# Statistics further ahead in stage 1, x loaded before the constants, and the output gate computed 16 rows ahead across the border to stage 3

## The chip, the core and the metric

The kernel runs on one core of a Trainium2 chip. The core has a matrix engine (TensorE, PE in the profile), a vector engine (VectorE, DVE), an activation engine (ScalarE, ACT), a general engine (GpSimd, POOL) and a queue engine that issues transfers (SyncE, SP). Each engine works through its own instructions in order, and the engines wait for one another through semaphores. The metric is the device time of one execution in microseconds (us); lower is better. A change counts as faster or slower here when the time moves by more than 2%.

## The reference, cut to what matters

x has 384 x 384 positions of 128 channels. Two layers are applied to it, in float32.

```python
# layer 0
z = layernorm(x)
left  = (z @ Wl + bl) * sigmoid(z @ Wlg + blg)
right = (z @ Wr + br) * sigmoid(z @ Wrg + brg)
core  = einsum('bikh,bjkh->bijh', left, right)      # for each channel h a 384x384x384 product
zo    = layernorm(core) @ Wout + bout
x     = x + sigmoid(x @ Wg + bg) * zo               # the gate uses the x that came in

# layer 1, on the new x (called pair)
left      = pair @ W_left + b_left + pair @ W_eq + b_eq
right_sum = sum over the row of (pair @ W_right + b_right)
gate      = sigmoid(pair @ W_gate + b_gate)
out       = (left * right_sum * gate) @ W_out + b_out
x         = layernorm(out + pair)
```

The gate `sigmoid(x @ Wg + bg)` of layer 0 needs only the kernel's input, not `core`.

## The kernel before

It has three stages, one after the other.

**Start.** 28 small loads (weights, biases) go out on SyncE's queue, the weights are folded with the norms' scales, and only then the first loads of x are issued.

**Stage 1** goes over x in 144 chunks of 8 rows of 128 positions. A chunk is two steps of four rows. Per step: statistics on VectorE, 1/sqrt(var+eps) by a power chain on GpSimd (once a chunk), scaling on GpSimd, four transposes on TensorE, four projections onto 512 columns, a sigmoid on ScalarE, a product on VectorE. Slices of the result go to DRAM.

```python
AHEAD = NQ + 3                       # NQ = 2 steps a chunk
def stats(n, q, half):
    for r in range(r0, r0 + 2):
        seq(nc.vector.bn_stats(st[:, r, :], loaded[n][:, r, :]))
    for r in range(r0, r0 + 2):
        seq(nc.vector.bn_aggr(mv[:, r, :], st[:, r, :]))
    if q == NQ - 1 and half == 1:    # the power chain, once a chunk
        seq(nc.gpsimd.tensor_scalar(rs, mv[:, :, 1], EPS, 1.0, ALU.add, ALU.mult))
        seq(nc.gpsimd.tensor_tensor(rs, rs, mhalf[:, :XR], ALU.pow))
        seq(nc.gpsimd.tensor_tensor(sh, mv[:, :, 0], rs, ALU.mult))
        seq(nc.gpsimd.tensor_scalar(sh, sh, -1.0, 1.0, ALU.mult, ALU.add))
...
for k, (n, q) in enumerate(steps):
    if k + 2 < len(steps):
        zs[k + 2] = scale(*steps[k + 2])          # GpSimd, four rows of z
    for half in range(2):
        back(n, q, zt, half)                      # projections, sigmoid, product
        if half == 0 and k + 1 < len(steps):
            ahead = front(zs.pop(k + 1))          # transposes, copy
        if k + AHEAD < len(steps):
            stats(*steps[k + AHEAD], half)
    ...
```

`seq` keeps an instruction behind those that were written before it for the same engine.

**Stage 2** goes over the 128 channels: 9 matmul pairs each, a copy to SBUF, the square, two running sums, and a store of `core`. After it, `rstd` is computed for three blocks of 128 rows, on VectorE and ScalarE (a square root), and stored.

**Stage 3** goes over 384 rows in a software pipeline. `tick(t)` works on row t-d for several delays d:

```python
# d=1: gate matmul, sigmoid           d=0: three transposes of x, copy, cs = core * rstd
# d=2: pr matmul, two vector ops      d=3: two matmuls, sigmoid, vector op
# d=6: wo on ScalarE                  d=7: six py matmuls, statistics
# d=9: normalize on ScalarE           d=10: scale and shift, store every 4 rows
load_rows(0); load_rows(RG)           # x, core and rstd of 4 rows each
for t in range(N + D):                # D = 10
    ...
    tick(t)
```

Of the kernel before, what the change touches and what calls it, by code (L numbers as in the profile page):

```python
# [19 lines left out]
def triangle_then_gated_row_kernel(ctx: ExitStack, tc: tile.TileContext, a: dict, out: bass.AP):  # L20
# [20 lines left out]
    RG = 4  # L41

# [10 lines left out]

    def const(shape, name):
        return cpool.tile(shape, F32, tag=name, name=name)

    def load(dst, src):
        nc.sync.dma_start(out=dst, in_=src)
# [11 lines left out]
    ident = const([P, P], "ident")  # L70
    make_identity(nc, ident)
    avg = const([P, P], "avg")
    nc.vector.memset(avg, 1.0 / P)
    mhalf = const([P, 16], "mhalf")
    nc.vector.memset(mhalf, -0.5)

    g0, b0 = column("L0_conv_norm_g"), column("L0_conv_norm_b")
    go, bo = column("L0_conv_onorm_g"), column("L0_conv_onorm_b")
    wout0, bout0 = matrix("L0_conv_Wout"), column("L0_conv_bout")
    wg0, bg0 = matrix("L0_conv_Wg"), column("L0_conv_bg")  # L80
    wleft, bleft = matrix("L1_conv_W_left"), column("L1_conv_b_left")
    weq, beq = matrix("L1_conv_W_eq"), column("L1_conv_b_eq")
    wright, bright = matrix("L1_conv_W_right"), column("L1_conv_b_right")
    wgate, bgate = matrix("L1_conv_W_gate"), column("L1_conv_b_gate")
    wout1, bout1 = matrix("L1_conv_W_out"), column("L1_conv_b_out")
    lns, lnb = const([P, C], "lns"), const([P, C], "lnb")
    load(lns, a["L1_conv_ln_scale"].partition_broadcast(P))
    load(lnb, a["L1_conv_ln_bias"].partition_broadcast(P))

    wz = const([P, 4 * H], "wz")  # L90
    wc = const([P, C], "wc")
    bz = const([P, 1], "bz")
    with tc.tile_pool(name="prep", bufs=1) as pp, tc.tile_pool(name="prep_ps", bufs=1, space=PSUM) as ps:

        wst, wcat = pp.tile([P, 4 * H], F32, name="wst"), pp.tile([P, 4 * H], F32, name="wcat")
        bst, bcat = pp.tile([1, 4 * H], F32, name="bst"), pp.tile([1, 4 * H], F32, name="bcat")
        for n, (w, b) in enumerate((("Wl", "bl"), ("Wr", "br"), ("Wlg", "blg"), ("Wrg", "brg"))):
            load(wst[:, n * H:(n + 1) * H], a["L0_conv_" + w])
            load(bst[:, n * H:(n + 1) * H], a["L0_conv_" + b].rearrange("(o h) -> o h", o=1))
        for t, st in ((wcat, wst), (bcat, bst)):  # L100
            for g in range(2):
                nc.vector.tensor_copy(
                    t[:, g * 2 * H:(g + 1) * 2 * H].rearrange("p (h s) -> p s h", s=2),
                    st[:, g * 2 * H:(g + 1) * 2 * H].rearrange("p (s h) -> p s h", s=2),
                )

        d = pp.tile([P, 1], F32, name="d")
        nc.vector.tensor_sub(d, b0, g0)  # L110
        m1 = pp.tile([P, P], F32, name="m1")
        nc.vector.tensor_scalar(m1, avg, d, None, ALU.mult)
        p1 = ps.tile([P, 4 * H], F32, name="p1")
        nc.tensor.matmul(p1, lhsT=m1, rhs=wcat, start=True, stop=False)
        nc.tensor.matmul(p1, lhsT=avg[0:1, :], rhs=bcat, start=False, stop=True)
        nc.vector.scalar_tensor_tensor(wz, wcat, g0, p1, ALU.mult, ALU.add)


        m2 = pp.tile([P, P], F32, name="m2")
        nc.vector.tensor_scalar(m2, avg, go, -1.0, ALU.mult, ALU.mult)  # L120
        p2 = ps.tile([P, C], F32, name="p2")
        nc.tensor.matmul(p2, lhsT=m2, rhs=wout0, start=True, stop=True)
        nc.vector.scalar_tensor_tensor(wc, wout0, go, p2, ALU.mult, ALU.add)
        p3 = ps.tile([P, 1], F32, name="p3")
        nc.tensor.matmul(p3, lhsT=wout0, rhs=bo, start=True, stop=True)
        nc.vector.tensor_add(bz, p3, bout0)


        nc.vector.tensor_add(wleft, wleft, weq)
        nc.vector.tensor_add(bleft, bleft, beq)  # L130
        p4 = ps.tile([P, 3], F32, name="p4")
        for n, w in enumerate((wleft, wgate, wright)):
            nc.tensor.matmul(p4[:, n:n + 1], lhsT=w, rhs=bout1, start=True, stop=True)
        for n, b in enumerate((bleft, bgate, bright)):
            nc.vector.tensor_sub(b, b, p4[:, n:n + 1])
        nc.vector.tensor_scalar(bright, bright, float(N), None, ALU.mult)


    chunks = [(kb, ig, c) for kb in range(NB) for ig in range(NG) for c in range(G // XR)]
    kept = {(NB - 1, ig): None for ig in range(NG - KEEP, NG)}  # L140
    with ExitStack() as ctx2:
# [15 lines left out]
        with tc.tile_pool(name="p1x", bufs=6) as xp, tc.tile_pool(name="p1w", bufs=3) as wp, \  # L157
             tc.tile_pool(name="p1s", bufs=5) as sp, \
# [3 lines left out]
            AHEAD = NQ + 3  # L162
# [13 lines left out]

            def stats(n, q, half):

# [10 lines left out]
                if q == NQ - 1 and half == 1:  # L189
                    seq(nc.gpsimd.tensor_scalar(rs, mv[:, :, 1], EPS, 1.0, ALU.add, ALU.mult))  # L190
                    seq(nc.gpsimd.tensor_tensor(rs, rs, mhalf[:, :XR], ALU.pow))  # L191
                    seq(nc.gpsimd.tensor_tensor(sh, mv[:, :, 0], rs, ALU.mult))
                    seq(nc.gpsimd.tensor_scalar(sh, sh, -1.0, 1.0, ALU.mult, ALU.add))
# [56 lines left out]
            for n in range(6):  # L250
                load_chunk(n)
# [3 lines left out]
            zs = {k: scale(*steps[k]) for k in range(2)}  # L255
            zt = front(zs.pop(0))
            for k, (n, q) in enumerate(steps):
                ahead = None
                if k + 2 < len(steps):
                    zs[k + 2] = scale(*steps[k + 2])  # L260
                for half in range(2):
                    back(n, q, zt, half)
                    if half == 0 and k + 1 < len(steps):
                        ahead = front(zs.pop(k + 1))
                    if k + AHEAD < len(steps):
                        stats(*steps[k + AHEAD], half)
# [4 lines left out]
                store_slice()  # L271
                if k == len(steps) - 2 * G // 4 + 16:
# [5 lines left out]
        spool = ctx2.enter_context(tc.tile_pool(name="stats", bufs=1))  # L278
        with tc.tile_pool(name="p2out", bufs=3) as op, tc.tile_pool(name="p2sq", bufs=2) as qp, \
             tc.tile_pool(name="p2ps", bufs=2, space=PSUM) as ps:  # L280
# [34 lines left out]
        with tc.tile_pool(name="rstd", bufs=2) as rp:  # L315
            for b in range(NB):
                m2, ve, r0, r1 = (rp.tile([P, N], F32, tag=t, name=t) for t in ("m2", "ve", "r0", "r1"))
                nc.vector.scalar_tensor_tensor(m2, csum[:, b], 1.0 / (H * H), csum[:, b], ALU.mult, ALU.mult)
                nc.vector.scalar_tensor_tensor(ve, csq[:, b], 1.0 / H, m2, ALU.mult, ALU.subtract)
                nc.vector.tensor_scalar(ve, ve, 0.0, EPS, ALU.max, ALU.add)  # L320
                nc.scalar.activation(r1, ve, AF.Sqrt)
                nc.vector.reciprocal(r0, r1)
                nc.vector.tensor_mul(r1, r0, r0)
                nc.vector.scalar_tensor_tensor(r1, r1, -0.5, ve, ALU.mult, ALU.mult)
                nc.vector.scalar_tensor_tensor(r1, r1, 1.5, r0, ALU.add, ALU.mult)
                nc.sync.dma_start(out=rstd_d[b * P:(b + 1) * P, :], in_=r1)

    with tc.tile_pool(name="p3in", bufs=3) as inp, tc.tile_pool(name="p3out", bufs=3) as op, \
         tc.tile_pool(name="p3w", bufs=4) as wp, tc.tile_pool(name="p3l", bufs=7) as lp, \
         tc.tile_pool(name="p3s", bufs=4) as sp, \
         tc.tile_pool(name="p3ps", bufs=4, space=PSUM) as ps, \
         tc.tile_pool(name="p3ps2", bufs=4, space=PSUM) as ps2:
# [8 lines left out]

        nc.vector.tensor_scalar(lns, lns, -1.0, None, ALU.mult)
        lnsb = lns.unsqueeze(1).to_broadcast([P, NB, C])
        lnbb = lnb.unsqueeze(1).to_broadcast([P, NB, C])
        loaded, rows, yts, pair, quad = {}, {}, {}, {}, {}

        def load_rows(i0):  # L350
            if i0 < N:
                xt = inp.tile([P, RG, NB, C], F32, tag="xt", name="xt")
                seq(nc.sync.dma_start(out=xt, in_=x[i0:i0 + RG].rearrange("i (b p) c -> p i b c", p=P)))
                ct = inp.tile([P, RG, N], F32, tag="ct", name="ct")
# [6 lines left out]
                loaded[i0] = xt, ct, rt  # L361

        D = 10

        def tick(t):

            r = [rows.get(t - d) for d in range(D + 1)]
            if r[1]:

                pg = bank("pg")  # L370
                seq(nc.tensor.matmul(pg[:, :N], lhsT=wg0, rhs=r[1]["xT"], start=True, stop=True))  # L371
                gT = r[1]["gT"] = work("gT")
                seq(nc.scalar.activation(gT, pg[:, :N], AF.Sigmoid, bias=bg0))
            if r[0]:
# [128 lines left out]
```

## Time and profile before

The time is 3588.69 us, the median of three runs (3588.11 to 3588.82). The profiled execution has a span of 3585.8 us.

| stretch of the profiled execution | us | TensorE counted busy |
| --- | --- | --- |
| start, until the first projection at 30.2 us | 30.2 | |
| stage 1, 30.0 to 1238.5 | 1208.5 | 1180.1 |
| stage 2, 1239.9 to 2020.0 | 780.1 | 779.8 |
| border, 2019.7 to 2039.4 | 19.7 | 0.9 |
| stage 3, 2060 to 3550 | 1490.0 | 1490.0 |
| after the last matmul, 3571.9 to 3586.0 | 14.1 | 0.0 |

In the lines that follow below, a timeline's columns are the start and the duration in us, the engine, the line of the kernel, the operation, what it writes and reads, and how often; in brackets the idle time before it and what ended it. PE is TensorE, SPq SyncE's queue. In a list of waits the columns are the total in us, the number of times and the longest. TensorE's busy time is to be read with care, since the ends of matmuls are modelled: a start is better evidence than a duration.

### The profile page before, as it was taken

To read this page: it belongs to the slowest core of one execution; us is meant where nothing else is said; L and a number is where in the kernel's file an instruction comes from. 1 tells how busy PE (TensorE), PEld (TensorE's weight loads), DVE (VectorE), ACT (ScalarE), POOL (GpSimd) and SP (SyncE) were. 2 spreads that over 40 slices of the span, in tenths; PEclk is the share of its full clock that TensorE was granted. 3 is DMA by queue.
4 is the path that set the end of the run, shared out by engine and by line. 5 is a ranking of instruction groups with operands and counts; after the bars stand their busy time and mean duration, and the time that the engine had idled before them with its cause. 6 is when DMAs were issued, how large, how long until landed. Compare 5 with 4: busy or idle time off the path is not lost.

```text
span 3585.8 us, 48072 instructions
## 1 busy us (share of the span) xinstructions
PE 3496.5 (98%) x13646; PEld 2102.3 (59%) x13646; DVE 2357.0 (66%) x7498; ACT 1962.6 (55%) x3815; POOL 1997.5 (56%) x3526
## 2 busy tenths in 40 slices
PE   7999999999999999999999799999999999999997
PEld 3444444444444455555555477777777777777775
DVE  4666666666666544444444588888888888888886
ACT  2444444444444333333333377777777777777776
POOL 4666666666666500000000167777777777777776
PEclk9999999999999999999999899999999999999999
DMA  3675675675675288888888766666666666666662
GB/s 86 178 222 164 182 219 162 183 219 162 186 219 158 76 271 268 270 268 273 270 266 271 240 197 205 194 201 204 194 202 199 198 203 198 199 203 196 202 203 89
DMA packets 885056, 726.00 MB, mean 202 GB/s; under 512 B 18484, under 2 KB 823352, under 8 KB 884792
## 3 DMA queue, kind: packets, MB, share of 16 engines
q1 hardware_dynamic: 884792, 722.94, 65.2%
q8 instruction: 110, 1.80, 0.2%
q14 instruction: 154, 1.26, 0.1%
HBM read 437.07 MB, written 285.80 MB: 202 GB/s over the span
## 4 chain that ended last, share of the span: by engine, by line
PE 73%; POOL 16%; DVE 6%; ACT 3%; issue 2%; DMA 0%; SPq 0%; POOLq 0%; DVEq 0%; ACTq 0%
PE pc L299 22%; PE pr L233 7%; PE pr L405 7%; PE py L434 7%; PE pg L371 7%; PE pl L420 7%; PE pg L419 7%; POOL z L201 7%; POOL rs L191 7%; PE pxt L378 4%; PE py L435 3%; DVE lr L237 3%; ACT sg L235 2%; DVE st L186 2%; PE pt L210 1%
## 5 line engine op out<-in xcount | busy, mean ns | idle before, releaser
L233 PE MATMUL pr<-wz,zt 128*128 128x512 f32 x2304 | 1038.9, 594 | 0.7 <-ACT zt L212 0.7
L299 PE MATMUL pc<-lrh 128*128 128x384 f32 x2304 | 779.8, 499 | 1.4 <-DVE lr L237 1.4
L237 DVE TENSOR_TENSOR lr<-pr,sg 128x512 f32<-128x512 f32 x576 | 398.3, 691 | 471.6 <-ACT sg L235 471.6
L235 ACT ACTIVATE sg<-pr 128x512 f32<-128x512 f32 x576 | 344.0, 597 | 643.3 <-PE pr L233 327.7
L233 PEld LDWEIGHTS pr<-wz,zt 128*128 128x128 f32 x2304 | 424.1, 194 | 415.0 <-issue 414.0
L299 PEld LDWEIGHTS pc<-lrh 128*128 128x128 f32 x2304 | 446.9, 194 | 334.5 <-DVE lr L237 2.2
L455 ACT ACTIVATE py<-py,nm,rs 128x128 f32<-128x128 f32 x1152 | 495.5, 430 | 117.2 <-POOL rs L449 90.3
L201 POOL TENSOR_SCALAR z<-xt,rs,sh 128x128 f32<-128x128 f32 x1152 | 500.4, 458 | 0.0
L308 DVE TENSOR_TENSOR csum<-csum,ct 128x1152 f32<-128x1152 f32 x128 | 173.8, 1358 | 445.0 <-ACT ct L305 445.0
L290 POOL COPY lrh<-lr 128x128 f32<-128x128 f32 x256 | 68.1, 296 | 705.4 <-issue 694.4
L434 PEld LDWEIGHTS py<-wo,u 128*128 128x128 f32 x2304 | 378.5, 191 | 105.9 <-ACT py L455 2.9
L382 POOL TENSOR_TENSOR cs<-ct,rt 128x384 f32<-128x384 f32 x384 | 384.1, 1001 | 46.6 <-DMA rt<-rstd_d 40.8
L305 ACT COPY ct<-pc 128x1152 f32<-128x1152 f32 x128 | 143.3, 1120 | 486.3 <-PE pc L299 486.3
L434 PE MATMUL py<-wo,u 128*128 128x128 f32 x2304 | 404.5, 275 | 4.3 <-ACT py L455 2.7
L391 POOL TENSOR_TENSOR yt<-yt,lnb 128x384 f32<-128x384 f32 x384 | 384.0, 1000 | 5.1 <-DVE yt L388 5.1
L440 DVE BATCH_NORM_STATS2 st<-py 128x6 f32<-128x128 f32 x1152 | 266.1, 286 | 114.7 <-PE py L435 114.7
L371 PE MATMUL pg<-xT,mat_L_conv_Wg 128*128 128x384 f32 x768 | 313.3, 490 | 11.8 <-ACT xT L380 11.8
L405 PE MATMUL pr<-cs,wc 128*128 128x384 f32 x768 | 319.8, 498 | 0.0
L406 DVE SCALAR_TENSOR_TENSOR pr<-pr,bz,gT 128x384 f32<-128x384 f32 x384 | 240.2, 625 | 116.6 <-PE pr L405 116.0
L435 PE MATMUL py<-ident,x1T 128*128 128x128 f32 x1152 | 314.7, 273 | 0.0
L419 PE MATMUL pg<-x1T,mat_L_conv_W_gate 128*128 128x384 f32 x768 | 310.5, 486 | 0.0
L420 PE MATMUL pl<-x1T,mat_L_conv_W_left 128*128 128x384 f32 x768 | 310.5, 486 | 0.0
(85 smaller groups left out, 4778.1 us busy)
## 6 DMA issues: line engine op xcount, KB each, us to landing
lr_d<-lr SPq DMA_DIRECT2D x128, 1024.0 KB, 9.1
lrh<-lr_d SPq DMA_DIRECT2D x128, 768.0 KB, 4.9
xt<-in_x_dram SPq DMA_DIRECT2D x144, 512.0 KB, 5.2
core_d<-ct SPq DMA_DIRECT2D x128, 576.0 KB, 6.2
xt<-in_x_dram SPq DMA_DIRECT2D x96, 768.0 KB, 5.0
ct<-core_d SPq DMA_DIRECT2D x96, 768.0 KB, 8.8
rt<-rstd_d SPq DMA_DIRECT2D x96, 768.0 KB, 6.3
out_dram<-yt SPq DMA_DIRECT2D x96, 768.0 KB, 4.1
```

Source lines behind the costliest of these rows:

```text
L201: seq(nc.gpsimd.tensor_scalar(z[:, r, :], xt[:, rr, :], rs[:, rr:rr + 1], sh[:, rr:rr + 1], ALU.mult, ALU.add))
L233: seq(nc.tensor.matmul(pr[:, r, :], lhsT=zt[:, 2 * half + r, :], rhs=wz, start=True, stop=True))
L235: seq(nc.scalar.activation(sg, pr[:, :, 2 * H:], AF.Sigmoid))
L237: seq(nc.vector.tensor_tensor(t[:, :, i0:i0 + 2, :], pr[:, :, :2 * H].rearrange("k i (h s) -> k h i s", s=2), sg.rearrange("k i (h s) -> k ...
L299: seq(nc.tensor.matmul(pc[:, ib, :N], lhsT=t[:, kb, ib * P:(ib + 1) * P, 0], rhs=t[:, kb, :, 1], start=(kb == 0), stop=(kb == NB - 1),))
L371: seq(nc.tensor.matmul(pg[:, :N], lhsT=wg0, rhs=r[1]["xT"], start=True, stop=True))
L405: seq(nc.tensor.matmul(pr[:, :N], lhsT=wc, rhs=r[2]["cs"], start=True, stop=True))
L419: seq(nc.tensor.matmul(pg2[:, :N], lhsT=wgate, rhs=r[3]["x1T"], start=True, stop=True))
L420: seq(nc.tensor.matmul(pl[:, :N], lhsT=wleft, rhs=r[3]["x1T"], start=True, stop=True))
L434: seq(nc.tensor.matmul(py[:, s], lhsT=r[7]["u"][:, s], rhs=r[7]["wo"], start=True, stop=False))
L435: seq(nc.tensor.matmul(py[:, s], lhsT=r[7]["x1T"][:, s], rhs=ident, start=False, stop=True, is_transpose=True))
L455: seq(nc.scalar.activation(py[:, s], py[:, s], AF.Identity, bias=nm[:, n, b:b + 1], scale=rs[:, n, b:b + 1]))
```

## The change

It has five parts:

1. In stage 1 the statistics run one step further ahead (`AHEAD = NQ + 4`), and the power chain is taken out of `stats` and put behind the scaling of its step, one step after the statistics that it reads. It is meant to keep GpSimd from waiting for VectorE with finished work behind it.
2. The first six loads of x are issued before anything else, and the constants are loaded through ScalarE's queue, those of stage 1 first. The folding of the weights for stage 3 is moved into stage 1, after its step 20.
3. In stage 3 the transposes of x and the gate run 16 rows ahead of the rest (A = 16), so that they can start before `rstd` is there. x is loaded apart from core and rstd. The pipeline becomes D = 26 ticks long.
4. `rstd` is computed inside stage 3, after row 4, in two passes over the three blocks, and stored through GpSimd's queue.
5. The pools of stages 2 and 3 wait for the tiles whose bytes they take over, not for the whole pool before them (`reuse_waits="tile"`), and lie on the other side of SBUF where that is needed. The output of the last four rows is stored row by row.

The diff, cut to its core ("..." where lines are left out):

```diff
+    A = 16
...
     def load(dst, src):
-        nc.sync.dma_start(out=dst, in_=src)
+        seq(nc.scalar.dma_start(out=dst, in_=src))
...
-            AHEAD = NQ + 3
+            AHEAD = NQ + 4
...
+            for n in range(6):
+                load_chunk(n)
...  (the constants of stage 1, ident, avg, the folding of wz)
+            def weights():
+                seq(nc.vector.scalar_tensor_tensor(wz, wcat, g0, p1[:, 0], ALU.mult, ALU.add))
...  (the loads of the other constants)
+            def late_weights():
+                ps = tps.tile([P, 4, P], F32, tag="pt", name="pw")
+                m2 = wp.tile([P, 4, C], F32, tag="z", name="m2")[:, 0]
+                seq(nc.vector.tensor_scalar(m2, avg, go, -1.0, ALU.mult, ALU.mult))
+                seq(nc.tensor.matmul(ps[:, 0], lhsT=m2, rhs=wout0, start=True, stop=True))
+                seq(nc.vector.scalar_tensor_tensor(wc, wout0, go, ps[:, 0], ALU.mult, ALU.add))
...
+                for n, (w, b) in enumerate(((wleft, bleft), (wgate, bgate), (wright, bright))):
+                    p4 = ps[:, 2, n:n + 1]
+                    seq(nc.tensor.matmul(p4, lhsT=w, rhs=bout1, start=True, stop=True))
+                    seq(nc.vector.tensor_sub(b, b, p4))
...
-                if q == NQ - 1 and half == 1:
+            def powers(n, q):
+                if q == NQ - 1:
+                    _, mv, rs, sh = normed[n]
                     seq(nc.gpsimd.tensor_scalar(rs, mv[:, :, 1], EPS, 1.0, ALU.add, ALU.mult))
...
             for k in range(AHEAD):
                 for half in range(2):
                     stats(*steps[k], half)
-            zs = {k: scale(*steps[k]) for k in range(2)}
-            zt = front(zs.pop(0))
+                if k == 1:
+                    weights()
+                if k < AHEAD - 1:
+                    powers(*steps[k])
+                if k == 1:
+                    zs = {j: scale(*steps[j]) for j in range(2)}
+                    zt = front(zs.pop(0))
             for k, (n, q) in enumerate(steps):
                 ahead = None
                 if k + 2 < len(steps):
                     zs[k + 2] = scale(*steps[k + 2])
+                if k + AHEAD - 1 < len(steps):
+                    powers(*steps[k + AHEAD - 1])
...
+                if k == 20:
+                    late_weights()
...
+        with tc.tile_pool(name="p2out", bufs=3, side="right", reuse_waits="tile") as op, \
+             tc.tile_pool(name="p2ps", bufs=2, space=PSUM, reuse_waits="tile") as ps:
...
+        xip, fp, inp, op = pool("p3x", 4), pool("p3f", A + 4), pool("p3in", 3), pool("p3out", 3)
...
+        def rstd():
...  (for all three blocks: variance on VectorE, square root on ScalarE; then for all three:)
+                seq(nc.vector.reciprocal(m, r))
...
+                seq(nc.gpsimd.dma_start(out=rstd_d[b * P:(b + 1) * P, :], in_=r))
...
-        D = 10
+        D = A + 10
...  (in tick: gate at delay 1 and transposes at delay 0 as before, cs at delay A,
...   everything else at its old delay plus A)
-        load_rows(0)
-        load_rows(RG)
+        for i0 in range(0, 4 * RG, RG):
+            load_x(i0)
         for t in range(N + D):
+            if t == 5:
+                rstd()
+                load_core(0)
+                load_core(RG)
...
+            if i >= N - RG:
+                seq(nc.sync.dma_start(
+                    out=y[i].rearrange("(b p) c -> p b c", p=P), in_=yts[N - RG][:, i % RG]
+                ))
```

## The prediction, made before the change was run

> **What bounds the kernel now.** I read the page's busy table first, then the slices, then the timeline of TensorE inside each stage, and last the list of waits. The busy table says that TensorE works all the time:
>
> ```profile
> PE 3496.5 (98%) x13646; PEld 2102.3 (59%) x13646; DVE 2357.0 (66%) x7498; ACT 1962.6 (55%) x3815; POOL 1997.5 (56%) x3526
> ```
>
> If that were true there would be 2% to win. But a matmul's end is modelled, so I looked at starts. The timeline of TensorE in the middle of stage 1:
>
> ```profile
> 503.52 1.24 PE L210 MATMUL pt<-ident,z 128*128 128x128 f32 x4
> 504.60 3.60 PE L233 MATMUL pr<-wz,zt 128*128 128x512 f32 x8
> 508.03 0.60 PE L210 MATMUL pt<-ident,z 128*128 128x128 f32 x4
> 508.47 3.60 PE L233 MATMUL pr<-wz,zt 128*128 128x512 f32 x8
> 511.90 1.23 PE L210 MATMUL pt<-ident,z 128*128 128x128 f32 x4
> 512.97 3.60 PE L233 MATMUL pr<-wz,zt 128*128 128x512 f32 x8
> ```
>
> The first column is the start, the second the duration. Eight projections take 3.43 us from start to the next group, always. Four transposes take 0.44 us from their start to the projections (508.03 to 508.47) in one step and 1.08 us (503.52 to 504.60) in the next. The long ones are counted as busy and are in truth waiting in between. The timeline of all engines there shows that z is written at one row per 0.44 us by POOL, just ahead of each transpose. Why POOL is late stands in the waits of stage 1 (30 to 1238 us):
>
> ```profile
> POOL rs L190 <- DVE mv L188: 349.6, 142, 6.7
> ```
>
> 142 times, once a chunk, POOL stands still for 2.46 us (349.6/142) at the power chain (four operations, 508.54 to 511.02, so 2.5 us), because the statistics end late on DVE; the z rows that TensorE needs next are queued behind that chain. A chunk is two steps: 8.38 us (508.03 to 516.41 in the same timeline). Without the wait it would be 2 x (0.44 + 3.43) = 7.74 us. So 0.64 us per chunk is lost.
>
> Stage 2 has nothing of the kind: 128 channels in 780 us (1239.9 to 2020), 6.09 us each, TensorE dense. Stage 3 neither: four rows take 15.85 us (3.96 each), and TensorE has no idle time from 2060 to 3550. Left are the start, where the first projection comes at 30.2, the border to stage 3, and the drain of some 14 us after the last matmul (3571.8 of 3585.8). The timeline of the start and of the border, cut:
>
> ```profile
> 13.16 30.59 SPq L172 DMA_DIRECT2D xt<-in_x_dram  x8
> 27.74 1.78 PE L210 MATMUL pt<-ident,z 128*128 128x128 f32 x4 [8.85 <-POOL z L201]
> 30.20 3.78 PE L233 MATMUL pr<-wz,zt 128*128 128x512 f32 x4 [0.68 <-ACT zt L212]
> ...
> 2021.36 0.43 SPq L353 DMA_DIRECT2D xt<-in_x_dram  x1
> 2027.34 0.88 PE L378 MATMUL pxt<-ident,xt 128*128 128x128 f32 x3 [7.63 <-DMA xt<-in_x_dram]
> 2039.43 1.65 PE L371 MATMUL pg<-xT,mat_L_conv_Wg 128*128 128x384 f32 x2 [11.21 <-ACT xT L380]
> 2042.28 1.65 PE L371 MATMUL pg<-xT,mat_L_conv_Wg 128*128 128x384 f32 x2 [0.57 <-ACT xT L380]
> 2044.36 1.56 PE L405 MATMUL pr<-cs,wc 128*128 128x384 f32 x2
> ```
>
> The first x load is issued only at 13.16, behind 28 constant loads. At the border TensorE waits 7.6 us for x and 11.2 us because ScalarE's copy stands behind the third square root, and it then runs at half rate.
>
> **What the Trainium skill says.** (1) "TensorE: Matmul & The Clock Gate", Part 1: after an idle window of about 3.4 us the array is gated to half its clock, and about as long a busy spell frees it. The trace agrees: the gate's matmul pair takes 1.65 us at 2039.4 and 0.81 us in steady state, and recovery takes some 6 us here. (2) The same page's table at the top: the queues of ScalarE, VectorE and GpSimd are strict FIFO. The trace agrees: finished x rows do not overtake the power chain on POOL. So order alone can cure stage 1. (3) The same page, Part 4: a transpose does not count as TensorE activity for that gate. No view of this trace shows it; it matters for a rival below. (4) "Trainium Kernel Development and Optimization", Key Constraints: loads issued from several engines share the same DMA engines, so a second issuer saves issue time only. Here a constant costs 0.43 us of issue on SyncE, and that is just what stands ahead of x.
>
> **The change part by part.**
>
> *Stage 1's order.* Statistics run one step further ahead (lead 6 instead of 5), and the power chain for a chunk is placed behind the scaling of its step and one step after its statistics. I count time in steps of 3.87 us. DVE ends a step's statistics about half a step after TensorE has left that step (508.45 against about 506.3). Under the new order the chain in even step k needs statistics of step k-1, ready at k+0.55; it takes 0.63 steps, so until about k+1.15; the z rows behind it take 0.45 steps, until k+1.6; TensorE wants them at k+2.45. That is 0.85 steps, over 3 us, of slack where there was a deficit of 0.64 us. POOL's work per chunk is 8 x 0.44 + 2.5 = 6.0 of 7.74 us; DVE's is 4 x 1.3 = 5.2; ScalarE's about 3.6. Nothing else becomes the bound. The gain: (1233 - 43)/8.38 = 142 chunks x 0.64 = **-90 us**.
>
> *x before constants.* Loads of x go out at about 0.7 us instead of 13.16. The projection then waits for: ten constants issued on ScalarE's queue (0.7 + 10 x 0.47 = 5.4), landed by about 8.5 (2 us as before, 1 more for the x traffic); the copies and m1, 9.2; statistics of two steps 2.35, so 11.6; chain 2.5, so 14.1; first z, cold transposes and copy (27.23 to 30.20 before, 3.0 us), so about 17. Against 30.2: **-13 us**.
>
> *Late weights.* The preparation for stage 3, which lay in the wait at the start, now comes at step 20 in the middle of a dense stage: six small matmuls and ten DVE operations in turns, in one PSUM bank. TensorE first waits for DVE to finish its backlog of half a step, about 2 us, then some five round trips of 0.6 to 1 us (at 4.53 to 5.60 the first one took 1.1). I put it at **+7 us**.
>
> *Border to stage 2.* The 1.4 us wait for the last write of lr can go, since PSUM waits by tile: **-1 us**.
>
> *Border to stage 3.* The first x load is still issued behind the last store of core (program order on SyncE), so the 7.6 us stay. Then gate and transposes of rows 0 to 15 run, with the rstd work after row 4, and the first main-path matmul (pr) comes in tick 18. In these ticks TensorE has only 0.33 + 0.65 = 0.98 us of work, but there is a chain: gate matmul to sigmoid 0.84, sigmoid to copy 0.48, copy 0.48, to the next matmul 0.05, so 1.85 us (starts at 2160.77, 2161.61 and 2162.09 in steady state). About four cold ticks at 2.85 (2039.43 to 2042.28) and twelve at 1.85 are 33.6; tables and three square roots 4; ticks 17 and 18 some 3 us more; less half a tick for the first. So pr of row 0 comes about 7.6 + 39 = 47 us after stage 2's end, against 24.6 before (2044.36 - 2019.7): +22 us. The rstd results are long there by then. It is paid back at the end: the last 16 rows need no gate and no transposes. TensorE would need 2.98 us a row; DVE needs about 3.4 (3.9 less its waits of 0.3 + 0.3), so 16 x 0.55 = -9 us. The last store is per row, 192 KB instead of 768 KB: -2 to -3 us. Together **+10 us**: the work is moved into a place where TensorE idles, but at ScalarE's pace and at the price of a later start of the main path.
>
> Sum: 3588.7 - 90 - 13 + 7 - 1 + 10 = **3502 us**, of which stage 1 ends near 1145, stage 2 near 1926.
>
> **The rivals.** *A new wait in stage 1 takes back much of the 90 us.* For it: stores and loads already saturate the DMA in half of each group (348 GB/s at 516 to 520), the group shrinks from 67 to 62 us, and statistics want x a step earlier. Against: landing of x takes 10.8 us at most, the load goes out when POOL has finished with the buffer, about six steps (23 us) ahead, and the other half of the group is nearly free (10 to 130 GB/s). It would give some 3530. *The gate runs fast.* If the 16 rows went at TensorE's own 0.98 us, the border would be about 14 us shorter, and the whole near 3485; the strict order sigmoid, copy on ScalarE speaks against it. *The gate runs cold.* With TensorE half idle, and transposes not counted, the clock may stay at half: 12 more ticks at +1.0, so 3514. *Throttling of a denser stage 1*: stage 3 is dense for 1490 us at a granted clock of 1.00, so no.
>
> **Range and chances.** Stage 1's gain is read directly from starts and I give it +-5; start and late weights together +-7, the border +-12. So 3480 to 3525. The 2% line is 3517; it takes a cold border and a slow start together, or a new wait in stage 1, to miss it: faster by over 2% 0.87, within 0.12, slower 0.01.
>
> **What will show it.** In stage 1 every group of transposes should stand 0.44 us ahead of its projections, a chunk take 7.75 us, and the wait of POOL for DVE shrink. The first projection should start near 17. A gap of several us should stand once, some 100 us in. After stage 2 a row of gate matmuls at 1.8 to 2.9 us spacing should precede the first pr by some 35 us or more, and the last 16 rows should go at about 3.4 us. It is wrong if transposes still wait every second step, if DVE waits for x, or if the border is shorter than before.

## The result, and the profile after

The changed kernel takes 3529.38 us (median of four runs, 3527.08 to 3531.18) against 3588.76 us for the kernel before. The ratio is 0.9834, with a 95% interval of 0.9817 to 0.9851: 1.7% faster, so within 2%. The prediction was 3502 us with a range of 3480 to 3525; the result lies above the range, 27 us above the estimate.

The page's busy table of the changed kernel again gives TensorE 98% of a now shorter span:

```profile
PE 3460.8 (98%) x13646; PEld 2109.6 (60%) x13646; DVE 2355.9 (67%) x7498; ACT 1946.6 (55%) x3815; POOL 1994.4 (57%) x3529
```

As before, this row tells nothing. The starts do. TensorE's timeline in the middle of stage 1 (start, duration, engine, line, operation):

```profile
502.25 0.60 PE L226 MATMUL pt<-ident,z 128*128 128x128 f32 x4
502.68 3.60 PE L249 MATMUL pr<-wz,zt 128*128 128x512 f32 x8
506.12 0.60 PE L226 MATMUL pt<-ident,z 128*128 128x128 f32 x4
506.56 3.60 PE L249 MATMUL pr<-wz,zt 128*128 128x512 f32 x8
```

Every group of transposes now stands 0.44 us ahead of its projections; the long ones of 1.08 us are gone, and a step takes 3.87 us. Yet GpSimd's wait for the statistics has shrunk by only a quarter. From the list of waits of stage 1 (total us, times, longest), the line that answers to "349.6, 142, 6.7":

```profile
POOL rs L206 <- DVE mv L199: 264.9, 141, 9.7
```

GpSimd still stands still for 1.9 us in every chunk. What changed is when the wait ends. GpSimd's timeline, the chain's first operation and the z rows behind it, before (first two lines) and after:

```profile
508.54 0.20 POOL L190 TENSOR_SCALAR rs<-mv 128x8 f32<-128x8 f32 x1 [2.43 <-DVE mv L188]
511.01 3.47 POOL L201 TENSOR_SCALAR z<-xt,rs,sh 128x128 f32<-128x128 f32 x8
...
502.75 0.20 POOL L206 TENSOR_SCALAR rs<-mv 128x8 f32<-128x8 f32 x1 [1.82 <-DVE mv L199]
505.21 3.46 POOL L217 TENSOR_SCALAR z<-xt,rs,sh 128x128 f32<-128x128 f32 x8
```

Before, the first four rows behind the chain (from 511.01) were those of the transposes at 511.90, so TensorE waited for them. Now the first four rows (from 505.21) are those of the transposes at 509.99, and the last of them is written 3.0 us earlier. GpSimd's own order has not changed: from the third chain on, each chain has the same number of z rows ahead of it in both traces (12, then 8 more each time). Taking the chain out of `stats` only kept its place there while the statistics moved ahead. So it is VectorE's lead over the chain, one step more, that made the wait harmless.

The start, in the timeline of all engines of the changed kernel (x goes out first, on SPq; the constants on ACTq, of which the first eight are shown in part):

```profile
0.72 24.35 SPq L106 DMA_DIRECT2D xt<-in_x_dram  x7
2.31 0.31 ACTq L58 DMA_DIRECT2D stage<-in_L_conv_br_dram  x1
5.22 0.34 ACTq L58 DMA_DIRECT2D stage<-in_L_conv_Wlg_dram  x1
9.08 0.33 ACTq L58 DMA_DIRECT2D stage<-in_L_conv_Wrg_dram  x1
15.06 0.69 DVE L133 COPY stage<-stage 128x256 f32<-128x256 f32 x3 [7.38 <-DMA stage<-in_L_conv_Wrg_dram]
24.64 3.78 PE L249 MATMUL pr<-wz,zt 128*128 128x512 f32 x4 [1.15 <-ACT zt L228]
```

The constants' issue is held up twice (2.31 to 5.22, 5.60 to 9.08), and the last weight, issued at 9.08, is there only just before 15.06. VectorE works in order, so the statistics of x, which stand behind these copies, start only at 16.05. The first projection starts at 24.64 instead of 30.20. ScalarE's queue as such is not slow: from 2 to 14 us the DMA engines move 238 to 298 GB/s, from 14 to 16 us 12 GB/s, and from 15.09 on the same queue issues a constant about every 0.48 us.

TensorE's timeline at step 20, where the late weights stand in the middle of stage 1, cut:

```profile
106.57 0.60 PE L226 MATMUL pt<-ident,z 128*128 128x128 f32 x4
107.01 1.88 PE L249 MATMUL pr<-wz,zt 128*128 128x512 f32 x4
111.13 0.46 PE L171 MATMUL pw<-mat_L_conv_Wout,m 128*128 128x128 f32 x2 [2.24 <-issue]
...
115.37 3.66 PE L249 MATMUL pr<-wz,zt 128*128 128x512 f32 x4
118.87 0.60 PE L226 MATMUL pt<-ident,z 128*128 128x128 f32 x4
```

From the transposes at 106.57 to these at 118.87 it is 12.3 us instead of 3.87, a hole of 8.4 us. It ends with projections at half rate: four in 3.66 us, where four took 1.88 at 107.01.

And the border to stage 3, TensorE's timeline, cut:

```profile
1939.96 0.87 PE L418 MATMUL pxt<-ident,xt 128*128 128x128 f32 x3 [7.92 <-DMA xt<-in_x_dram]
1941.73 1.65 PE L410 MATMUL pg<-xT,mat_L_conv_Wg 128*128 128x384 f32 x2 [0.90 <-ACT xT L420]
1943.17 0.85 PE L418 MATMUL pxt<-ident,xt 128*128 128x128 f32 x3
1944.59 1.65 PE L410 MATMUL pg<-xT,mat_L_conv_Wg 128*128 128x384 f32 x2 [0.57 <-ACT xT L420]
...
1989.49 1.65 PE L410 MATMUL pg<-xT,mat_L_conv_Wg 128*128 128x384 f32 x2 [0.57 <-ACT xT L420]
1992.35 1.65 PE L410 MATMUL pg<-xT,mat_L_conv_Wg 128*128 128x384 f32 x2 [0.57 <-ACT xT L420]
1994.42 1.49 PE L453 MATMUL pr<-cs,wc 128*128 128x384 f32 x2
```

A pair of gate matmuls takes 1.65 us in the first tick and still 1.65 in the last, 0.81 in steady state (from the pair's start to the next group's, 1.44 us against 0.64): the clock stays at half ("cold" below, against "warm" for full) through all 16 rows, at 2.86 us a tick. The view of busy time by stretches says the same. Its columns are the stretch, its length, the busy time of TensorE, its weight loads, VectorE, ScalarE and GpSimd with their instructions, then the granted clock, the DMA share and GB/s:

```profile
1939.96:1994.40 54.44, 41.81 (x93) 21.75 (x94) 12.82 (x13) 22.65 (x41) 5.74 (x7) 0.50 0.63 194
```

TensorE is counted busy for 41.81 of 54.44 us there, at a granted clock of 0.50.

The balance, each term the difference of two starts in the two profiled executions (spans 3585.8 and 3525.9):

| from ... to | before | after | change | predicted |
| --- | --- | --- | --- | --- |
| start to first projection | 30.20 | 24.64 | -5.6 | -13 |
| first projection to stage 2 (its start at 1239.92, 1152.24) | 1209.7 | 1127.6 | -82.1 | -90 + 7 - 1 |
| stage 2 | 779.8 | 779.8 | 0 | 0 |
| stage 2's end to row 0's main path (2019.71 to 2044.36; 1932.04 to 1994.42) | 24.6 | 62.4 | +37.7 | +22 |
| from there to the end | 1541.4 | 1531.5 | -9.9 | -11 to -12 |

The sum is -59.9, the difference of the spans. Of the last line, 2.4 us lie after the last matmul (11.7 us instead of 14.1), where the last rows are now stored one by one.

### The profile page after: what moved, and what is told of

Same layout as the page of the kernel before. It is cut to its first block, busy times and chain, and to the rows that moved or that the text cites. A ratio compares the mean times of both kernels' runs of the same rounds, so it can differ in the third digit from the quotient of the medians.

```text
span 3525.9 us, 48083 instructions
## 1 busy us (share of the span) xinstructions
PE 3460.8 (98%) x13646; PEld 2109.6 (60%) x13646; DVE 2355.9 (67%) x7498; ACT 1946.6 (55%) x3815; POOL 1994.4 (57%) x3529
## 4 chain that ended last, share of the span: by engine, by line
PE 96%; DVE 1%; ACT 1%; DMA 1%; issue 0%; POOL 0%; ACTq 0%; POOLq 0%; SPq 0%
PE pr L249 28%; PE pc L325 22%; PE pg L410 8%; PE pr L453 7%; PE py L485 7%; PE pg L469 7%; PE pl L470 7%; PE pxt L418 4%; PE pt L226 4%; PE py L486 3%; DMA xt<-in_x_dram 1%; ACT py L507 0%; PE pq L443 0%; POOL rs L496 0%; ACT xT L420 0%
## 5 line engine op out<-in xcount | busy, mean ns | idle before, releaser
L325 PE MATMUL pc<-lrh 128*128 128x384 f32 x2304 | 779.8, 499 | 1.4 <-DVE lr L253 1.4
L249 PEld LDWEIGHTS pr<-wz,zt 128*128 128x128 f32 x2304 | 416.6, 191 | 415.5 <-issue 414.1
L410 PE MATMUL pg<-xT,mat_L_conv_Wg 128*128 128x384 f32 x768 | 326.7, 508 | 12.6 <-ACT xT L420 12.6
```

The costliest lines, as they stand in the source:

```text
L249: seq(nc.tensor.matmul(pr[:, r, :], lhsT=zt[:, 2 * half + r, :], rhs=wz, start=True, stop=True))
L325: seq(nc.tensor.matmul(pc[:, ib, :N], lhsT=t[:, kb, ib * P:(ib + 1) * P, 0], rhs=t[:, kb, :, 1], start=(kb == 0), stop=(kb == NB - 1),))
L410: seq(nc.tensor.matmul(pg[:, :N], lhsT=wg0, rhs=r["xT"], start=True, stop=True))
```

## The experiments

The question was which of the five parts carries the gain, and what at the border and the start eats 30 us of it. Theory A: the clock stays at half because TensorE has gaps in the ticks with gate work alone. Theory B: the chain over ScalarE or rstd sets the border's length and the clock only follows. Executions of one and the same kernel differ by up to some 5 us (stage 2, with the same matmuls and waits, takes 783.6 us instead of 779.8 in the profiled execution of two of these runs), so differences of a few us are read from the traces.

### The order of stage 1 alone

```diff
 # the kernel before
-            AHEAD = NQ + 3
+            AHEAD = NQ + 4
     (power chain out of stats into powers(n, q), as in the change)
+                if k + AHEAD - 1 < len(steps):
+                    powers(*steps[k + AHEAD - 1])      # behind scale(k + 2)
```

> The kernel before with the new order of stage 1 alone (statistics one step further ahead, power chain behind the scaling). If that order is the whole gain, the time falls by 90 us or more, to about 3498, below the changed kernel's 3529, and the other four parts together cost 30 us. If the x loads first or the new pools carried part of the gain, it stays above 3529.

Measured: 3495.18 us, ratio 0.9741 (0.9727 to 0.9756). This one part is faster than the whole change by 34 us. Its first projection starts at 27.64 (the first power chain no longer waits for all statistics), stage 2 at 1146.49, so stage 1 takes 1118.9 us instead of 1209.7: 90.9 us less. The lines of these two starts:

```profile
27.64 3.78 PE L235 MATMUL pr<-wz,zt 128*128 128x512 f32 x4 [0.68 <-ACT zt L214]
...
1146.49 13.81 PE L306 MATMUL pc<-lrh 128*128 128x384 f32 x40 [1.41 <-DVE lr L239]
```

So part 1 carries the whole gain, and the other four parts together cost 34 us. Against this run's trace the changed kernel loses 37.8 us at the border and 8.8 in stage 1 (nearly all of it the hole of the late weights), and wins 10.8 at the tail and 3.0 at the start (24.64 against 27.64): +32.8, the difference of the two spans. Part 1 makes two edits, but since GpSimd's order here too is that of the kernel before, they come to one: the statistics lead the chain by one step more.

### A matmul to fill the gaps

```diff
 # the changed kernel, in tick, after the copy of xT
+                if 0 < t < A + 2:
+                    fl = ps2.tile([P, 512], F32, tag="py", name="fl")
+                    seq(nc.tensor.matmul(fl[:, :N], lhsT=wg0, rhs=row(1)["xT"], start=True, stop=True))
```

> The changed kernel with one more gate matmul pair (result unused) in each of ticks 1 to 17. Theory A, a cold clock: TensorE has too little matmul work there, so its clock stays at half; with the filler it warms after some 7 us, a tick falls from 2.85 to about 1.9 us, row 0's main path starts some 10 us earlier, and the total falls to about 3518. Theory B, the chain over ScalarE sets the pace whatever the clock: the filler gives nothing or lengthens a tick by its own 0.7 us, total 3529 to 3540.

Measured: 3515.0 us, ratio 0.9797 (0.9781 to 0.9813), 14 us faster than the changed kernel with more work in it. TensorE's timeline:

```profile
1940.88 1.65 PE L410 MATMUL pg<-xT,mat_L_conv_Wg 128*128 128x384 f32 x2 [0.90 <-ACT xT L420]
1942.33 0.85 PE L418 MATMUL pxt<-ident,xt 128*128 128x128 f32 x3
1942.97 1.24 PE L423 MATMUL fl<-xT,mat_L_conv_Wg 128*128 128x384 f32 x2
1944.04 0.81 PE L410 MATMUL pg<-xT,mat_L_conv_Wg 128*128 128x384 f32 x2
...
1954.72 1.65 PE L410 MATMUL pg<-xT,mat_L_conv_Wg 128*128 128x384 f32 x2 [3.04 <-ACT xT L420]
```

After one tick without a gap (3.2 us, 1940.88 to 1944.04) the pair is at 0.81 us, and a tick takes 1.95. The pause of 3.04 us at the square roots (1954.72) throws it back to 1.65 at once, and this time it takes two ticks, 6.4 us, until the pair at 1961.09 is at 0.81 again. Row 0's main path starts 50.4 us after stage 2 instead of 62.4. Theory A holds for these 12 us: once the clock is up, the chain over ScalarE lets a tick go in nearly the 1.85 us that the prediction gave it. The other 26 us over the kernel before are not the clock's: the 16 rows stand ahead of row 0 at any clock.

### Transposes as plain matmuls

```diff
 # the changed kernel, in tick, for the first A + 2 ticks
-                    seq(nc.tensor.transpose(pxt[:, s], r["x"][:, b, :], ident))
+                    seq(nc.tensor.matmul(pxt[:, s], lhsT=r["x"][:, b, :], rhs=ident, start=True, stop=True))
```

> The changed kernel with the transposes of the first 18 rows written as plain float32 matmuls against the identity (same result, two passes instead of one, and no transpose mode). If the clock stays cold because transposes do not count as activity, it warms and a tick falls below 2.2 us. If it stays cold because of the idle gap of 0.57 us in every tick, the gate's matmuls still take 1.65 us a pair and a tick gets longer, about 3.3 us.

Measured: one run, 3525.68 us. For 25 us (1943.4 to 1968.3) the pair stays at 1.65 us and a tick takes 3.5; then it warms, and stays warm, at 2.15 us a tick with the same gap of 0.57 us:

```profile
1959.92 1.65 PE L410 MATMUL pg<-xT,mat_L_conv_Wg 128*128 128x384 f32 x2 [0.57 <-ACT xT L423]
...
1968.34 0.91 PE L410 MATMUL pg<-xT,mat_L_conv_Wg 128*128 128x384 f32 x2 [0.57 <-ACT xT L423]
```

That is neither expectation. The transposes' kind is not the first cause, since with plain matmuls too the gate's pair stayed cold six times. Why it warmed at 1968 with the gaps still there stays open; the stretch between two gaps was longer here, 2.9 us instead of 2.3.

### Transposes to fill the gaps

```diff
 # the changed kernel, in place of the filler matmul
+                    for _ in range(2):
+                        for b, s in enumerate(cols):
+                            seq(nc.tensor.transpose(fl[:, s], r["x"][:, b, :], ident))
```

> The changed kernel with the gap of ticks 1 to 17 filled by six more transposes of x (result unused) instead of a matmul pair. If the clock needs only a TensorE without gaps, it warms as it did with the matmul filler, and a tick falls to about 1.9 us, total near 3515. If transposes do not count as activity, the gate's pair stays at 1.65 us, a tick is about 3.4 us, and the total is about 3537.

Measured: one run, 3515.49 us, as with the matmul filler. TensorE's timeline, cut:

```profile
1942.34 1.65 PE L410 MATMUL pg<-xT,mat_L_conv_Wg 128*128 128x384 f32 x2 [0.90 <-ACT xT L420]
...
1944.42 1.49 PE L425 MATMUL fl<-ident,xt 128*128 128x128 f32 x6
1945.70 1.39 PE L410 MATMUL pg<-xT,mat_L_conv_Wg 128*128 128x384 f32 x2
...
1948.13 0.91 PE L410 MATMUL pg<-xT,mat_L_conv_Wg 128*128 128x384 f32 x2
```

Transposes bring the clock up as matmuls do. In both runs it came up when the gap was filled; that the gap alone decides is not shown, since the run with plain matmuls warmed with its gaps.

### Fewer rows ahead

```diff
 # the changed kernel
-    A = 16
+    A = 6
```

> The changed kernel with A = 6 instead of 16, one number. By theory A each row of run-ahead costs 2.85 us at the border and gives back about 0.6 us at the end; rstd and core for row 0 are there about 38 us after stage 2, so row 0's main path starts at about 38 us instead of 62.4. Total 3529 - 24 + 6 = 3511. If the border is bound by something that does not depend on A, such as rstd, it stays at 3529.

Measured: 3510.93 us, ratio 0.9785 (0.9771 to 0.98), as expected. Row 0's main path starts 37.6 us after stage 2 instead of 62.4, and now it is the product of core and rstd that ends the wait; its line in TensorE's timeline:

```profile
1969.85 1.65 PE L453 MATMUL pr<-cs,wc 128*128 128x384 f32 x2 [3.61 <-POOL cs L426]
```

So 6 rows are enough to reach rstd; the other 10 only stood in its way. In the changed kernel that product was ready 25 us before it was used (1969.6 against 1994.4).

### rstd ahead of the ticks

```diff
 # the changed kernel
-    A = 16
+    A = 4
-            if t == 5:
-                rstd(); load_core(0); load_core(RG)
+        rstd()                                   # ahead of the loop over ticks
     # in rstd:
-                seq(nc.gpsimd.dma_start(out=rstd_d[b * P:(b + 1) * P, :], in_=r))
+                seq(nc.sync.dma_start(out=rstd_d[b * P:(b + 1) * P, :], in_=r))
+                if b == 0:
+                    load_core(0)
+                    load_core(RG)
```

> The changed kernel with rstd computed ahead of the first tick (square roots while x is in flight, the first block stored and read back at once on SyncE's queue) and A = 4. Row 0's main path should start about 24 us after stage 2 (62.4 in the changed kernel), with four rows of gate done by then, which is worth 3.9 us of TensorE's work, and the tail gives back 4 x 0.6 us: 3529 - 38 + 7 = 3498. If the border is bound elsewhere, it stays above 3511, the result of A = 6.

Measured: 3498.71 us, ratio 0.975 (0.9736 to 0.9765), 30.7 us less than the changed kernel. The square roots run while x is in flight (1939.0 to 1942.4; x is there at 1941.5), and row 0's main path starts 25.7 us after stage 2: 36.6 us won at the border and 6.9 given back at the end. Fewer rows alone gave 24.8 of the 36.6 (A = 6 above); how the rest is shared between rstd's place and its queue is not separated. That is still no better than the 24.6 of the kernel before, but four rows of gate are done by then.

### The constants of stage 1 ahead of x

```diff
 # the changed kernel
-        seq(nc.scalar.dma_start(out=dst, in_=src))
+        seq(nc.sync.dma_start(out=dst, in_=src))
     (the first six x loads moved behind Wl, Wr, Wlg, Wrg, their biases and the norm's scale and bias)
```

> The changed kernel with the ten constants that stage 1 needs ahead of the x loads, the other eighteen behind them, all on SyncE's queue. If the constants are late because 3 MB of x share the DMA with them, they land by 8 us, the first projection starts near 17.5 instead of 24.6, and the time falls by 7 us to 3522. If the start is bound by the statistics or by ScalarE's issue, nothing moves.

Measured: 3520.74 us, ratio 0.9813 (0.9797 to 0.983), 8.6 us less by the medians, 7.6 by the spans of the two traces. The first projection starts at 16.89, 7.75 us earlier. The last weight, issued at 2.98, is copied at 4.80, less than 2 us later, where it took almost 6 us beside the x traffic; its own issue had been held back by another 6. The run moves the constants to SyncE's queue too; that the traffic and not the queue held them back is read from the changed kernel's start above.

### The late weights in stage 2

```diff
 # the changed kernel
-                if k == 20:
-                    late_weights()
     # in stage 2's loop over channels h, with a bank of PSUM of their own:
+                # h == 4: the VectorE work that needs no matmul
+                # h == 6: all five matmul pairs, one after the other
+                # h == 8: the VectorE work that reads them
```

> The changed kernel with the late weights taken out of stage 1's step 20 and spread over channels 4, 6 and 8 of stage 2, so that TensorE and VectorE never take turns. The hole of 8.4 us at step 20 goes, some 1.5 us of small matmuls come into stage 2: 3529 - 7 = 3522.

Measured: 3520.1 us, ratio 0.9811 (0.9796 to 0.9826), 9.3 us less by the medians, 7.8 by the spans of the two traces. The five pairs now take 1.03 us (1186.09 to 1187.12) and nothing waits.

### Together, and with no rows ahead

The three mended parts in one kernel, first with A = 4, then with A = 0, then with A = 4 and the filler of the second experiment.

> The three mended parts together (constants of stage 1 ahead of x, late weights in stage 2, rstd ahead of the ticks with A = 4), with the new order of stage 1. If they are independent, the gains add: 3529.4 - 8.6 - 9.3 - 30.7 = 3481. If they share something, it stays nearer to the best of them, 3499.

> The same with A = 0, so no run-ahead at all. If running the gate ahead is worth its 0.98 us of TensorE's work per row while rstd is on its way, this is 2 to 4 us slower than with A = 4. If the run-ahead costs as much as it saves once the clock is cold, the two are equal.

> The version with A = 4 and the unused gate matmul in ticks 1 to 5. The filler brought 14 us with 16 rows ahead because the cold ticks were on the path. Here rstd is on the path, and only the last one or two ticks are, so it should bring 1 to 4 us; if it brings nothing, the clock no longer matters at this border.

| kernel | us | ratio to the kernel before (95%) | row 0's main path after stage 2 |
| --- | --- | --- | --- |
| A = 4 | 3484.12 | 0.9707 (0.9692 to 0.9721) | 25.8 |
| A = 0 | 3483.03 | 0.9706 (0.9689 to 0.9722) | 22.2 |
| A = 4, filler | 3479.57 | 0.9694 (0.968 to 0.9708) | 22.2 |

The gains nearly add (3481 expected, 3484 measured). Without the filler, running ahead is worth nothing: with A = 0, TensorE waits 7.65 us for rstd but starts row 0 earlier by 3.6 us, since with A = 4 the last cold ticks of the rows ahead still stand in front of it. With the filler the four rows fit into rstd's shadow. The gain of 4.5 us over A = 4 is at the edge of what these times separate; the trace's 3.5 us at row 0 agrees with it. The last is the fastest kernel of the study, 3.1% below the kernel before and 50 us below the changed one.

## Why the prediction was right and wrong

The miss of 27 us is 15.7 at the border, 7.4 at the start, 1.9 in stage 1 and 1.6 at the end. A cold border together with a slow start was named as what would miss the 2% line, and given a chance of 0.12.

**Stage 1's order: right.** -90 predicted, -90.9 measured with this part alone. The reading from starts held, and so did the slack ("over 3 us"; the trace has 3.0), since the prediction's count goes by when the statistics are ready. What it concludes from the queues, "order alone can cure stage 1", does not fit: the order on GpSimd is as before, and the earlier statistics are the cure. One expected sign was weaker than forecast: the wait of GpSimd was to shrink, and it shrank only from 2.46 to 1.9 us a chunk. With the same work of 6.0 us in a chunk of 7.75 instead of 8.38 us, GpSimd must idle for the rest; what cost time was that the wait ended too late for the rows behind it.

**The border: the step that failed.** "About four cold ticks at 2.85 and twelve at 1.85" should have been all cold: twelve ticks at 1 us more, and the two ticks behind them cold as well instead of "some 3 us more". So row 0's main path started at +62.4 and not at +47; with the filler, and so with a warm clock in most ticks, it started at +50.4. The chain itself, 2.85 us a cold tick, was right to 0.01 us, and the square roots cost 2.1 us on top of their tick, not 4. The case was among the rivals ("The gate runs cold", +12), given as the less likely. The argument for it was wrong in one half: it named transposes that do not count, and the transposes as fillers show that they do count. The other half, that TensorE with too little to do keeps the clock down, fits, though TensorE was idle by the trace for a fifth of the time and not for half. The four cold ticks fit a recovery of some 6 us as in a dense stretch; in a stretch with a gap in every tick it did not come.

**The start: a term mis-sized.** The constants were to be there by 8.5 us with 1 us more for the x traffic; they were copied at 15.06. The line of thought (two issuers save issue time) left out that loads issued beside 3 MB of x are themselves held back, in their issue and in their landing. Putting ten small loads first costs x 4 us of issue and wins 7.75 at the first projection.

**Late weights: right** (+7 predicted, a hole of 8.4 measured, 7.8 won back in stage 2; there are five small matmuls, not six). **Border to stage 2: wrong** (-1 predicted, 0 measured): the wait for the last write of lr is still there, 1.4 us, so the pools that wait by tile won nothing at that place. **Tail: right** (-11 to -12 predicted, -9.9 measured; the last rows go at 3.47 us each, 13.87 for four). The prediction's own terms put the ends of stages 1 and 2 at about 1142 and 1923, not at its 1145 and 1926; measured are 1150.8 and 1932.0.

The Trainium skill, "TensorE: Matmul & The Clock Gate", Part 1, gives the full clock only after a sustained busy window of about 3.4 us. The changed kernel agrees: its busy stretches of 2.29 us (a tick of 2.86 less the gap of 0.57) left the clock at half for 54 us, and without gaps it was up after 3.2 to 6.4 us in the filler run. So the passage that the prediction quotes held the answer, and the gap of 0.57 us stood in its own line at 2042.28; it did not put the two together. The run with plain matmuls, which warmed between gaps, is not explained by it. For the way back Part 1 gives an idle window of about 3.4 us; here a pause of 3.04 us was enough. Its Part 4, that a transpose does not count as busy in the same way, is contradicted by the run with transposes as fillers: there the gate's own matmuls fill 1.44 us of a first tick of 3.36, a smaller share than the 1.44 of 2.86 that stayed cold, and the clock came up.

## What to carry to other kernels

In an in-order queue ask when a wait ends and when the work behind it is needed, not how long the wait is: statistics one step earlier were worth 90 us, though GpSimd keeps its order and still waits three quarters as long as before. Before work is pulled forward into a hole, look at the pace at which it can run there and at what it then keeps from starting: 16 rows at half clock pushed the main path back by 38 us and gave back at most 10 us. When several parts are changed at once, run the main one alone: here it was 34 us better than the whole.

## What the runs showed of the hardware

A TensorE whose work has one gap of 0.57 us in each 2.86 us stayed at half clock for 54 us (granted clock 0.50). With the gap filled, by matmuls or by transposes, the clock came up within two ticks (3.2 and 6.4 us in the run with the matmul filler), and a pause of 3.04 us took it down again. Once warm it stayed warm for 24 us with the same gap in each 2.15 us, in the run with plain matmuls; that run had warmed with a gap in each 3.5 us, and why stays open. Useless matmuls made a kernel 14 us faster. Small loads issued beside 3 MB of x took almost 6 us from issue to use, and less than 2 us when issued first.
